# Writing out the first rounds and the last rounds of a software pipeline: gated attention and a GAT layer over 64 graphs

## The chip, the cores and the metric

The kernel runs on one core of a Trainium2 chip. The metric is the device time of one execution in microseconds, the median of several runs. Engines are named as in the profile: PE (TensorE, matrix products), DVE (VectorE), ACT (ScalarE), POOL (GpSimd) and SP (SyncE, which here issues the DMA transfers). Each engine works through its own queue in order.

## What is computed

There are 64 graphs of 256 nodes with 512 features (`x`: 64 x 256 x 512) and an adjacency matrix each (`adj`: 64 x 256 x 256). Two layers, each with a residual:

```python
# layer 0: gated multi-head attention, 8 heads of 64
h = maximum(layernorm(x), 0)
q, k, v = h @ Wq.T, h @ Wk.T, h @ Wv.T
attn = softmax(where(adj != 0, q @ k.T / 8, -inf))
c = attn @ v
gate = sigmoid(concat([c, h]) @ Wg.T + bg)
x = x + gate * h + (1 - gate) * c
# layer 1: GAT
h = maximum(layernorm(x), 0)
Wh = h @ W
e = leaky_relu((Wh @ a1)[:, :, None] + (Wh @ a2)[:, None, :], 0.2)
attention = softmax(where(adj == 0, -1e9, e))
x = x + elu(attention @ Wh)
```

## The kernel before

All is in float32. A graph passes through the pipeline in four groups of steps, named by their first letter and by the round in which they run. In round `i` the kernel does the preparation of graph `p = i + 1` (`p_`), the attention of graph `i` (`a_`), gate and first half of the GAT layer of graph `q = i - 1` (`g_`), the GAT product and softmax of graph `r = i - 2` and the last elementwise steps and the store of graph `o = i - 3`. `emit_round` (L650) writes the order of these steps by hand; that order is the order of every engine's queue, because the kernel is built under a manual schedule (L814): nothing reorders it. `do(fn, g, ...)` leaves a step out when graph `g` doesn't exist, and so the rounds at both ends (-1, 0, 1, ... and 63 to 66) are the same list with holes in it.

The five large products of a graph (q/k together, v, gate, wh; L158 `strassen`) are done with seven block products instead of eight. A product is a list of steps: "1" to "7" are block products on PE into three PSUM banks (`ma`, `mb`, `mc`, one buffer each), "u1", "u2", "u3" are partial sums and "c00" to "c11" the results, on DVE or ACT (L185, L187). Bank a holds steps 1 and 2, bank b 6, 7 and 4, bank c 5 and 3; a step that adds to a bank whose partial sum is still to be read waits for that read. `run(fn, g, "1 u1 6 ...")` in `emit_round` spreads these steps over the round and remembers which of them are done. The operands' token sums (L146, four additions on POOL) come before a product, weight sums (L104, four on DVE a weight) once, at the start, some of them as "chores" spread over the first rounds.

The steps that matter here:

- `load_graph` (L89): x and adj of a graph, on SP. `load_weight` (L99): two DMAs of 512 KB a weight; at the start wq and wv go on SP, wk on ACT's queue.
- `p_stats`, `p_root`, `p_bias`, `p_norm` (L224 to L233): layernorm and relu; statistics on DVE, the root on POOL, the norm on ACT.
- `p_turn`, `p_send`, `p_fetch` (L257 to L269): transposes h to hT. For graphs 0 and 1 on PE with an identity matrix (`transpose_pe`, L275), then copies to SBUF on DVE and ACT. From graph 2 on: 32 x 32 blocks on DVE, then a DMA to DRAM and back, both issued on SP.
- `p_qk` (L303), `p_v` (L321), `a_scores` (L328): q/k and v products, and the 8 heads' scores, partly into banks b and c.
- `a_max` (L349, DVE), `a_exp` (L358, ACT), `a_scale` (L367, POOL for three quarters, ACT for one), `a_turn` (L379, DVE), `a_send` and `a_fetch` (SP, L399 and L404): softmax and transpose of the weights; `eT` is what is fetched. `a_weigh` (L410): attention times v, on PE; `a_evac` (ACT).
- `g_gate` (L442), `g_diff` (POOL), `g_tanh` (ACT), `g_mix` (DVE): the gate. `g_turn`, `g_residual`: back to rows and added to x. For graphs from `LAST` = 62 on, PE does the transposes.
- `g_stats` to `g_norm`, `g_turn_h`, `g_sums_h`, `g_wh` (L546): layer 1's norm and product. `g_edges` (L552, PE), `g_logits`, `g_leaky` (DVE), `g_exp` (ACT), `g_turn_e` (L587, from graph 61 on by PE): its softmax. `g_out` (L611, PE): attention times Wh.
- `g_neg` (DVE), `g_pos` (ACT, two activations), `g_elu` (DVE), `g_add` (L635, POOL), `g_store` (L639, SP): elu, residual, store.

Before the rounds, L814 to L822 load graph 0 and wq, wk, wv, and normalise and transpose graph 0. The kernel's rounds -1 to 66 follow.

Of the kernel before, what the change touches and what calls it, by code (L numbers as in the profile page):

```python
# [8 lines left out]
F32 = mybir.dt.float32  # L9
# [3 lines left out]
ALU = mybir.AluOpType  # L13
# [9 lines left out]
def kernel(  # L23
# [32 lines left out]
    nc = tc.nc  # L56
    B, N, H = x.shape
# [4 lines left out]
    NT = N // P  # L62
    HH = H // 2
    SCALE = 1.0 / DK ** 0.5
    LAST = B - 2
    assert N == 256 and H == 512 and SCALE == 0.125

    def pool(name, bufs, **kw):
# [20 lines left out]
    def load_graph(g):  # L89
        xt = sb["x"].tile([P, NT, H], F32, tag="t", name=f"x_{g}")  # L90
        at = sb["adj"].tile([P, NT, N], I32, tag="t", name=f"adj_{g}")
        nc.sync.dma_start(xt, x[g].rearrange("(t p) h -> p t h", p=P))
        nc.sync.dma_start(at, adj[g].rearrange("(t p) n -> p t n", p=P))
        graphs[g] = {"x": xt, "adj": at}

    weight = {}
    sources = {"q": wqT, "k": wkT, "v": wvT, "gc": wgT[:H], "gh": wgT[H:], "1": w1}

    def load_weight(key, eng):  # L99
        w = weight[key] = const.tile([P, HC, 2, HH + (key == "1")], F32, name=f"w{key}_sb")  # L100
        for n in range(2):
            eng.dma_start(w[:, :, n, :HH], sources[key][:, n * HH:(n + 1) * HH].rearrange("(c p) f -> p c f", p=P))

    def weight_sums(key):  # L104

        w = weight[key]
        t = const.tile([P, 3, 2, w.shape[3]], F32, name=f"w{key}_t")
        b11, b12, b21, b22 = (w[:, r:r + 2, n, :] for r in (0, 2) for n in range(2))
        weight[key] = {1: b11, 2: b21, 3: b22, 4: t[:, 2], 5: b12, 6: t[:, 0], 7: t[:, 1]}
        return [lambda args=args: nc.vector.tensor_tensor(*args) for args in (  # L110
            (t[:, 1], b22, b12, ALU.subtract),
            (t[:, 0], t[:, 1], b11, ALU.add),
            (b12, b12, b11, ALU.subtract),
            (t[:, 2], b21, t[:, 0], ALU.subtract),
        )]
# [140 lines left out]

    def p_turn(g):  # L257

        if g == 1:
            p_transpose_pe(g)  # L260
        elif g > 1:
            turn(graphs[g]["h"])

    def p_send(g):
        s = graphs[g]
        if g > 1:
            s["there"] = send_blocks(s.pop("h").rearrange("p t h -> p (t h)"), f"h_{g}")

    def p_fetch(g):  # L269
        s = graphs[g]  # L270
        if g > 1:
            s["hT"] = sb["hT"].tile([P, NT, HC, P], F32, tag="t", name=f"hT_l0_{g}")
            fetch_blocks(s["hT"], s.pop("there"))

# [129 lines left out]
    def a_fetch(g, half, jj):  # L404
        s = graphs[g]
        eT = sb["e"].tile([P, 4, 4 * NT, 32], F32, tag="t", name=f"eT_{g}_{half}_{jj}")
        fetch(eT.rearrange("p a n c -> p a (n c)"), s.pop(("there", half, jj)))
        s["eT", half, jj] = eT.rearrange("p a (i t k) c -> p i k t a c", i=2, t=NT)
# [15 lines left out]
    def a_evac(g, half):  # L424
        s = graphs[g]
        if half == 0:
            s["cT"] = sb["cT"].tile([P, NT, HC, P], F32, tag="t", name=f"cT_{g}")
        nc.scalar.copy(  # L428
            s["cT"][:, :, 2 * half:2 * half + 2, :].rearrange("p t j q -> p j t q"),
            s["pc"].rearrange("p j (t q) -> p j t q", q=P),  # L430
        )

    def a_sums(g):
        s = graphs[g]
        s["cS"] = token_sums(s["cT"], f"c_{g}")


    def g_sums(g):
        s = graphs[g]
        s["hS"] = token_sums(s["hT"], f"g_{g}")  # L440
# [61 lines left out]
    def g_residual(g, t):  # L502
        s = graphs[g]
        x = s["x"][:, t, :]
        if g >= LAST:
            nc.vector.tensor_tensor(x, x, s["py"][t], ALU.add)
        else:
            x = x.rearrange("p (j i c) -> p j i c", i=4, c=32)
            nc.vector.tensor_tensor(x, x, s["yT"][:, :, t].rearrange("p i j c -> p j i c"), ALU.add)

    def g_stats(g, t):
        norm_stats(graphs[g], t, f"l1_{g}")

    def g_root(g):
        norm_root(graphs[g], f"l1_{g}")

    def g_bias(g):
        norm_bias(graphs[g], f"l1_{g}")

    def g_norm(g):  # L520
        graphs[g]["h1"] = norm_relu(graphs[g], f"l1_{g}")
# [23 lines left out]

    def g_wh(g):  # L546
        s = graphs[g]
        s["wh"] = sb["wh"].tile([P, NT, 2, HH + 1], F32, tag="t", name=f"wh_{g}")
        dst = [[s["wh"][:, t, n, :] for n in range(2)] for t in range(2)]
        return strassen(f"wh_{g}", [P, HH + 1], on_tokens(weight["1"], s["h1S"]), dst)  # L550

    def g_edges(g):  # L552
        s = graphs[g]
        pe = s["pe"] = ps["w"].tile([P, N], F32, tag="t", name=f"pe_{g}")
        for t in range(NT):
            nc.tensor.transpose(pe[:, t * P:(t + 1) * P], s["wh"][:, t, 1, HH:].to_broadcast([P, P]), ident)

    def g_logits(g):
        s = graphs[g]
        e = s["eg"] = sb["tmp"].tile([P, NT, N], F32, tag="t", name=f"eg_{g}")  # L560
        for t in range(NT):
            nc.vector.scalar_tensor_tensor(
                e[:, t, :], s["pe"], s["wh"][:, t, 0, HH:], s["mask"][:, t, :], ALU.add, ALU.add
            )

    def g_leaky(g):
# [44 lines left out]
    def g_out(g, t):  # L611
        s = graphs[g]
        pm = s["po", t] = ps["w"].tile([P, H], F32, tag="t", name=f"po_{g}_{t}")
        for kc in range(NT):
            nc.tensor.matmul(  # L615
                pm, s["egT"][:, t, kc, :], s["wh"][:, kc, :, :HH], start=(kc == 0), stop=(kc == NT - 1)
            )

    def g_neg(g, t):
# [14 lines left out]

    def g_add(g, t):  # L635
        s = graphs[g]
        nc.gpsimd.tensor_tensor(s["x"][:, t, :], s["x"][:, t, :], s.pop(("pos", t)), ALU.add)  # L637

    def g_store(g):  # L639
        nc.sync.dma_start(out[g].rearrange("(t p) h -> p t h", p=P), graphs[g]["x"])  # L640


    products = {}
# [2 lines left out]
    def chore(steps, n):  # L646
        for _ in range(min(n, len(steps))):
            steps.pop(0)()

    def emit_round(i):  # L650
# [4 lines left out]
        def do(fn, g, *args):  # L655
            if 0 <= g < B:
                fn(g, *args)

        def run(fn, g, steps):
            if 0 <= g < B:  # L660
                if (fn, g) not in products:
                    products[fn, g] = fn(g), set()
                product, done = products[fn, g]
                for step in steps.split():
                    if step not in done:
                        product(step)
                        done.add(step)

        tail = i >= B - 1

        run(g_gate, q, "1")
        do(g_neg, o, 1)
        do(p_send, p)
# [9 lines left out]
        run(g_gate, q, "6 u2")  # L683
        do(a_turn, i, 0, 1, 1)
        do(a_send, i, 0, 1)
        do(g_sums_h, r)
        do(g_elu, o, 0)
        run(g_gate, q, "5")
        do(a_scale, i, 1, 0)
# [27 lines left out]
        do(g_mix, q, 1, False)  # L717
        chore(chores, 2)
        run(g_wh, r, "2 c00 4")
        do(p_sums, p)  # L720
        do(g_turn, q)
        do(g_send, q)
        do(a_fetch, i, 0, 1)
        run(g_wh, r, "c10 3 c01")
        do(g_fetch, q)
        do(a_fetch, i, 1, 0)

# [33 lines left out]
        chore(chores, 1)  # L761
        do(g_stats, q, 0)
        if i == -1:
            chore(weight_sums("v"), 4)
        run(p_v, p, "1 u1 6 u2")
        do(g_stats, q, 1)
        do(g_root, q)
# [2 lines left out]
        do(g_norm, q)  # L770
        run(p_v, p, "2 c00")
        chore(chores, 1)
        if not tail:
            do(g_turn_h, q)
            do(g_send_h, q)
        run(p_v, p, "4 c10")
        chore(chores, 1)
        run(p_v, p, "3 c01")
        chore(chores, 1)
        do(p_stats, p + 1, 0)  # L780
        do(p_stats, p + 1, 1)
        do(p_root, p + 1)
        do(g_sums, i)
        if tail:
            do(g_out, r, 0)
            do(g_out, r, 1)
            do(g_turn_h, q)

        do(a_weigh, i, 0)
        do(a_evac, i, 0)  # L790
        do(a_weigh, i, 1)
        do(a_evac, i, 1)
        do(a_sums, i)
        do(a_scores, p, 0)
        do(a_scores, p, 1)
        if not tail:
            do(g_out, r, 0)
            do(g_out, r, 1)
        do(a_max, p, 0, 0)
        do(p_bias, p + 1)  # L800
        do(a_exp, p, 0, 0, 0)
        do(a_max, p, 0, 1)
        do(a_exp, p, 0, 0, 1)
        do(p_norm, p + 1)
        do(a_max, p, 1, 0)
        do(a_max, p, 1, 1)
        do(g_fetch_h, q)
        do(a_scale, p, 0, 0)
        do(a_exp, p, 0, 1, 0)
        do(a_exp, p, 0, 1, 1)  # L810
        do(g_neg, r, 0)
        do(p_turn, p + 1)

    with tc.manual_schedule(engines={getattr(mybir.EngineType, e) for e in ("PE", "SP", "Pool", "DVE", "Activation")}):  # L814
        load_graph(0)
        load_weight("q", nc.sync)
        load_weight("k", nc.scalar)
        load_weight("v", nc.sync)
        p_stats(0, 0)
        p_stats(0, 1)  # L820
        for fn in (p_root, p_bias, p_norm, p_transpose_pe):
            fn(0)  # L822
        for i in range(-1, B + 3):
            emit_round(i)
            graphs.pop(i - 3, None)


# [30 lines left out]
```

## Time and profile before

| what | value |
|---|---|
| median of 3 runs | 3191.97 us (3191.17 to 3193.47) |
| the profiled execution's own time | 3185.72 us |
| its span on the core | 3183.9 us |
| PE busy | 3125.0 us (98% of the span) |
| PE weight loads busy | 2723.9 us (86%) |
| DVE, ACT, POOL busy | 2467.8, 1413.6, 1506.3 us (78%, 44%, 47%) |
| first matrix instruction on PE | 9.24 us |
| end of the last POOL addition, issue of the last store | 3180.06, 3180.08 us |

A row of the timeline reads: start in us, duration in us, engine, source line, operation, what it writes <- what it reads, shape, count; in brackets how long the engine had been idle and what released it. A row of waits reads: who waited, for whom, us in total, how many times, the longest. In a row of stages the busy time of each engine is followed by its number of instructions; the last three numbers are the clock granted to PE (1.00 is full), the share of the DMA engines and GB/s. Because PE is busy nearly throughout, what other engines do matters where PE waits for it.

### The profile page before, as it was taken

To read this page: it belongs to the slowest core of one execution; us is meant where nothing else is said; L and a number is where in the kernel's file an instruction comes from. 1 tells how busy PE (TensorE), PEld (TensorE's weight loads), DVE (VectorE), ACT (ScalarE), POOL (GpSimd) and SP (SyncE) were. 2 spreads that over 40 slices of the span, in tenths; PEclk is the share of its full clock that TensorE was granted. 3 is DMA by queue.
4 is the path that set the end of the run, shared out by engine and by line. 5 is a ranking of instruction groups with operands and counts; after the bars stand their busy time and mean duration, and the time that the engine had idled before them with its cause. 6 is when DMAs were issued, how large, how long until landed. Compare 5 with 4: busy or idle time off the path is not lost.

```text
span 3183.9 us, 66670 instructions
## 1 busy us (share of the span) xinstructions
PE 3125.0 (98%) x22716; PEld 2723.9 (86%) x22716; DVE 2467.8 (78%) x6366; ACT 1413.6 (44%) x3976; POOL 1506.3 (47%) x2183
## 2 busy tenths in 40 slices
PE   7899999999999999999999999999999999999997
PEld 6888888888889888888888898888888888888984
DVE  6777877877877878778778778778787787787774
ACT  2343543543544534435435445445344344454442
POOL 2454544544544545535445445445454454454453
PEclk9999999999999999999999999999999999999998
DMA  5678778777777777787787777777877877877761
GB/s 169 176 173 204 189 180 206 185 180 206 182 190 199 184 191 195 180 203 187 178 211 184 181 207 182 190 197 177 200 189 182 205 186 179 211 183 183 204 170 44
DMA packets 1103394, 590.63 MB, mean 186 GB/s; under 512 B 685776, under 2 KB 1029328, under 8 KB 1103056
## 3 DMA queue, kind: packets, MB, share of 16 engines
q1 hardware_dynamic: 1102000, 585.32, 73.9%
q8 instruction: 182, 2.98, 0.4%
q14 instruction: 156, 1.28, 0.1%
q10 hardware_dynamic: 1056, 1.05, 0.1%
HBM read 304.88 MB, written 281.28 MB: 184 GB/s over the span
## 4 chain that ended last, share of the span: by engine, by line
PE 90%; DVE 4%; POOL 2%; DMA 2%; issue 1%; SPq 1%; ACT 0%; DVEq 0%; POOLq 0%; ACTq 0%
PE pmb_qk L174 11%; PE pmb_z L174 9%; PE pc L418 7%; PE pma_qk L174 7%; PE pmc_qk L174 7%; PE ps L338 6%; PE po L615 6%; PE pma_z L174 6%; PE pmc_z L174 6%; PE pmb_v L174 5%; PE pmb_wh L174 5%; PE pma_v L174 3%; PE pmc_v L174 3%; PE pmc_wh L174 3%; PE pma_wh L174 3%; DVE e L353 1%
## 5 line engine op out<-in xcount | busy, mean ns | idle before, releaser
L362 ACT ACTIVATE e<-e,low 128x256 f32<-128x256 f32 x1024 | 506.5, 499 | 63.3 <-DVE low L353 63.3
L204 POOL TENSOR_TENSOR rs_l<-ve_l,mhalf 128x2 f32<-128x2 f32 x128 | 89.0, 695 | 869.7 <-DVE ve_l L200 869.7
L353 DVE CUSTOM_DVE_ANT_0 e<-ps,mask 128x256 f32<-128x256 f32 x1024 | 362.1, 415 | 100.1 <-PE ps L338 100.1
L377 POOL TENSOR_SCALAR e<-e,rec 128x256 f32<-128x256 f32 x768 | 352.7, 477 | 148.8 <-DVE rec L370 100.4
L386 DVE STREAM_TRANSPOSE eb<-e 128x512 f32<-128x512 f32 x512 | 351.8, 696 | 76.7 <-POOL e L377 63.4
L213 ACT ACTIVATE h_l<-x,nb_l,rs_l 128x512 f32<-128x512 f32 x256 | 194.1, 805 | 212.4 <-DVE nb_l L208 123.5
L152 POOL TENSOR_TENSOR S_l<-hT_l 128x256 f32<-128x256 f32 x128 | 93.4, 730 | 395.9 <-DMA hT_l<-there_h 361.9
L637 POOL TENSOR_TENSOR x<-x,pos 128x512 f32<-128x512 f32 x128 | 160.1, 1272 | 229.3 <-DVE pos L633 229.3
L615 PE MATMUL po<-wh,egT 128*128 128x512 f32 x512 | 242.5, 617 | 2.1 <-ACT egT L598 2.1
L338 PE MATMUL ps<-qk 64*128 64x256 f32 x2048 | 238.9, 383 | 0.6 <-DVE v L185 0.6
L418 PE MATMUL pc<-eT,v 128*64 128x256 f32 x2048 | 235.9, 382 | 0.1
L338 PEld LDWEIGHTS ps<-qk 64*128 64x128 f32 x2048 | 193.1, 187 | 45.3 <-DVE ve_l L200 21.9
L418 PEld LDWEIGHTS pc<-eT,v 128*64 128x64 f32 x2048 | 141.3, 137 | 86.7 <-DMA eT<-there_e 16.3
L239 DVE STREAM_TRANSPOSE h_l<-h_l 128x512 f32<-128x512 f32 x248 | 167.8, 695 | 54.7 <-ACT h_l L213 54.7
L615 PEld LDWEIGHTS po<-wh,egT 128*128 128x128 f32 x512 | 94.3, 194 | 118.5 <-issue 95.1
L362 ACT ACTIVATION_READ_ACCUMULATOR e<-e,low 128x1 f32 x1024 | 194.8, 190 | 0.0
L196 DVE BATCH_NORM_STATS2 bs_l<-x 128x6 f32<-128x512 f32 x256 | 172.9, 675 | 5.4 <-DMA x<-in_x_dram 5.4
L461 ACT ACTIVATE z<-z,hbg 128x256 f32<-128x256 f32 x256 | 116.1, 502 | 105.9 <-DVE z L185 105.9
L456 POOL TENSOR_TENSOR d<-hT_l,cT 128x512 f32<-128x512 f32 x128 | 160.5, 1274 | 0.0
L428 ACT COPY cT<-pc 128x512 f32<-128x512 f32 x128 | 74.9, 585 | 184.5 <-PE pc L418 184.5
L174 PEld LDWEIGHTS pma_z<-hT_l,wgh_sb 128*128 128x128 f32 x1024 | 129.2, 192 | 30.4 <-issue 30.4
L174 PE MATMUL pma_qk<-hT_l,wq_sb 128*128 128x128 f32 x1024 | 139.6, 280 | 11.9 <-DMA hT_l<-there_h 10.1
(146 smaller groups left out, 7964.8 us busy)
## 6 DMA issues: line engine op xcount, KB each, us to landing
there_e<-eb SPq DMA_DIRECT2D x256, 512.0 KB, 3.4
eT<-there_e SPq DMA_DIRECT2D x1024, 128.0 KB, 3.9
there_h<-h_l SPq DMA_DIRECT2D x496, 128.0 KB, 3.3
hT_l<-there_h SPq DMA_DIRECT2D x496, 128.0 KB, 3.3
x<-in_x_dram SPq DMA_DIRECT2D x64, 512.0 KB, 4.0
out_dram<-x SPq DMA_DIRECT2D x64, 512.0 KB, 4.2
there_y<-y SPq DMA_DIRECT2D x62, 512.0 KB, 3.3
yT<-there_y SPq DMA_DIRECT2D x248, 128.0 KB, 3.4
```

Source lines behind the costliest of these rows:

```text
L174: nc.tensor.matmul(bank[key][(slice(None), *cols)], lhsT, rhs, start=first and i == 0, stop=last and i == len(todo) - 1, skip_group_check= ...
L196: nc.vector.bn_stats(bs, s["x"][:, t, :])
L213: nc.scalar.activation(h[:, t, :], s["x"][:, t, :], AF.Relu, bias=s["nb"][:, t:t + 1], scale=s["rs"][:, t:t + 1])
L239: nc.vector.transpose(h[:, t, :], h[:, t, :])
L338: nc.tensor.matmul(psc[jj, i][:, t, :], qk[r:r + DK, 0, jj, t * P:(t + 1) * P], qk[r:r + DK, 1, jj, :], start=True, stop=True,)
L353: nc.vector.tensor_tensor_reduce(s["e", half, jj][:, i, t, :], s["ps", half][jj, i][:, t, :], s["mask"][:, t, :], -SCALE, HUGE, ALU.add, A ...
L362: nc.scalar.activation(e, e, AF.Exp, bias=s["low", half][:, jj, i, t:t + 1], scale=-1.0, accum_out=s["sums", half][:, jj, i, t:t + 1],)
L377: nc.gpsimd.tensor_scalar(e, e, rec[:, i, t:t + 1], 1.0, ALU.mult, ALU.mult)
L386: nc.vector.transpose(s["eb", half, jj][:, :, 4 * i:4 * i + 4, :].rearrange("p b n c -> p n b c"), e)
L418: nc.tensor.matmul(pc[i * DK:(i + 1) * DK, jj, :].rearrange("p (t a c) -> p t a c", t=NT, c=32), s["v"][:, kc, hd * DK:(hd + 1) * DK], eT[ ...
L456: nc.gpsimd.tensor_tensor(d, s["hT"][:, :, js, :], s["cT"][:, :, js, :], ALU.subtract)
L615: nc.tensor.matmul(pm, s["egT"][:, t, kc, :], s["wh"][:, kc, :, :HH], start=(kc == 0), stop=(kc == NT - 1))
```

## The change

In the front:

- SP loads x of graph 0, wq, wk, then adj of graph 0, then wv; ACT's queue issues no load. While x loads, PE transposes the identity matrix 44 times into a PSUM tile that nobody reads (`wake_up`).
- The sums of wv are done on POOL.
- In round -1, statistics of graph 1 and the scores and softmax of graph 0 are put ahead of the product v of graph 0.
- In round 0, the token sums of graph 1 come first, and its products q/k and v stand in the places of gate and wh, which that round doesn't have.
- Graph 2 is transposed on PE too (`FIRST` = 3).

At the end, round 63 stops after the product wh of graph 61, and `emit_end` writes out all that is left, for graphs 60 to 63. The additions of graphs 60 to 63 go to DVE. In graph 63 the additions are two (x + pos, then + (neg - 1)), and each half is stored on its own. Its wh has two tiles of its own, in buffers that held q and k. Rounds 1 to 62 keep their order.

```diff
+        if g > 0:
+            load_edges(g)
+
+    def load_edges(g):
+        nc.sync.dma_start(graphs[g]["adj"], adj[g].rearrange("(t p) n -> p t n", p=P))
...
     def p_turn(g):
-        if g == 1:
+        if g < FIRST:
             p_transpose_pe(g)
...
     def g_add(g, t):
         s = graphs[g]
-        nc.gpsimd.tensor_tensor(s["x"][:, t, :], s["x"][:, t, :], s.pop(("pos", t)), ALU.add)
+        eng = nc.vector if g >= B - 4 else nc.gpsimd
+        eng.tensor_tensor(s["x"][:, t, :], s["x"][:, t, :], s.pop(("pos", t)), ALU.add)
+    def g_add_first(g, t):
+        s = graphs[g]
+        nc.vector.tensor_tensor(s["x"][:, t, :], s["x"][:, t, :], s["pos", t], ALU.add)
+    def g_add_last(g, t):
+        x = graphs[g]["x"][:, t, :]
+        nc.vector.scalar_tensor_tensor(x, graphs[g].pop(("neg", t)), -1.0, x, ALU.add, ALU.add)
...
         def run(fn, g, steps):
+            if fn is g_gate and i == 0:
+                fn, g = p_qk, p
+            elif fn is g_wh and i == 0:
+                fn, g = p_v, p
...
+        if i == 0:
+            do(p_sums, p)
         run(g_gate, q, "1")
...
-        do(p_sums, p)
+        if i != 0:
+            do(p_sums, p)
         do(g_turn, q)
         do(g_send, q)
         do(a_fetch, i, 0, 1)
         run(g_wh, r, "c10 3 c01")
+        if i == B - 1:
+            return
...
         if i == -1:
-            chore(weight_sums("v"), 4)
+            chore(weight_sums("v", nc.gpsimd), 4)
+            stats()
+            scores()
         run(p_v, p, "1 u1 6 u2")
...
+    def wake_up():
+        pt = ps["w"].tile([P, 4, P], F32, tag="t", name="awake")
+        for k in range(44):
+            nc.tensor.transpose(pt[:, k % 4, :], ident, ident)
+
+    def emit_end():
+        a, b, c, o = B - 1, B - 2, B - 3, B - 4
+        a_fetch(a, 1, 0)
+        a_fetch(a, 1, 1)
+        g_edges(c)
+        for t in range(NT):
+            g_residual(b, t)
+            g_stats(b, t)
+        g_root(b)
+        g_bias(b)
+        g_sums(a)
+        g_norm(b)
+        for half in range(2):
+            a_weigh(a, half)
+            a_evac(a, half)
+        g_turn_h(b)
+        a_sums(a)
+        g_logits(c)
+        g_leaky(c)
+        gate = g_gate(a)
+        for step in "1 u1 6 u2 5".split():
+            gate(step)
+        g_exp(c)
+        g_sums_h(b)
+        g_elu(o, 1)
+        g_add(o, 1)
+        g_add(o, 0)
+        g_store(o)
+        g_rec(c)
...
+        g_out(c, 0)
+        g_out(c, 1)
+        g_turn(a)
+        wh = g_wh(b)
...
+        for t in range(NT):
+            g_residual(a, t)
+            g_stats(a, t)
+        g_root(a)
+        for step in "6 u2 5".split():
+            wh(step)
+        g_bias(a)
+        g_norm(a)
+        for step in "7 u3 c11 2 c00 4 c10 3 c01".split():
+            wh(step)
+        g_edges(b)
+        g_turn_h(a)
+        g_sums_h(a)
+        g_logits(b)
+        g_leaky(b)
+        last = g_wh(a)
...
+        for t in range(NT):
+            g_elu(c, t)
+            g_add(c, t)
+        g_store(c)
+        for step in "7 u3 c11 2 c00".split():
+            last(step)
...
+        for t in range(NT):
+            g_elu(b, t)
+            g_add(b, t)
+        g_store(b)
+        for t in range(NT):
+            g_neg(a, t)
+            g_pos(a, t)
+            g_add_first(a, t)
+        for t in range(NT):
+            g_add_last(a, t)
+            g_store(a, t)
...
         load_graph(0)
         load_weight("q", nc.sync)
-        load_weight("k", nc.scalar)
+        load_weight("k", nc.sync)
+        load_edges(0)
+        wake_up()
         load_weight("v", nc.sync)
...
-        for i in range(-1, B + 3):
+        for i in range(-1, B):
             emit_round(i)
-            graphs.pop(i - 3, None)
+            graphs.pop(i - 4, None)
+        emit_end()
```

## The prediction

> **What bounds the kernel now.** I first cut the span into three stages at the score products of round 2 and of round 62, with the busy time of each engine and the granted clock (the last three columns are clock, DMA share and GB/s):
>
> ```profile
> span 3183.9 us, 66670 instructions
> ...
> core 0: us, PE busy (x) PEld busy (x) DVE busy (x) ACT busy (x) POOL busy (x), PEclk, DMA share, GB/s
> 0.00:171.80 171.80, 141.06 (x1024) 126.33 (x1024) 117.94 (x305) 56.83 (x162) 53.27 (x90) 0.96 0.63 172
> 171.80:3079.90 2908.10, 2903.75 (x21244) 2538.07 (x21242) 2297.17 (x5935) 1319.91 (x3720) 1413.12 (x2044) 1.00 0.77 190
> 3079.90:3183.90 104.00, 80.21 (x456) 59.46 (x454) 52.73 (x126) 36.84 (x94) 39.88 (x50) 0.90 0.24 70
> ```
>
> TensorE is full between the ends, at full clock, and only its waits count. One graph costs it, by the chain of work: q/k and gate 7 x 1.79 = 12.5 us each, v and wh 6.07 each, scores 3.65, weighing 3.60, edges 0.45, output product 3.64: 48.5; two weighings in the middle start 48.29 apart. Up to 171.8 it has done 4 q/k, 4 v, 3 scores, 3 weighings, 2 gates, one wh, one edges and 16 transposes (1.8): 129.4 us, so the front loses 42.4. After 3079.9, 71.3 us of such work remain (two gates 25.0, three wh 18.2, three edges 1.3, four output products 14.6, scores and weighing 7.2, 44 transposes 5.0): the end loses 32.7. The middle loses 2908.1 - 60 x 48.29 = 10.7. The change can only reach for 75 us.
>
> Then who TensorE waited for, in the front and in the end (us, times, longest):
>
> ```profile
> PE pt_l L281 <- ACT h_l L213: 11.2, 4, 9.2
> PE pma_qk L174 <- DMA hT_l<-there_h: 6.3, 2, 6.0
> PE pmb_qk L174 <- POOL S_l L153: 4.0, 1, 4.0
> ```
> ```profile
> PE ptr L596 <- ACT eg L578: 9.6, 4, 3.2
> PE po L615 <- ACT egT L598: 2.1, 3, 0.7
> ```
>
> The front waits for its first input, for hT of graph 2 by DMA, for token sums of graph 1 behind two head scalings on POOL. The end waits three times for a GAT softmax. The clock by stretches shows what waits cost further:
>
> ```profile
> 39.03:42.44 3.41, 2.07 (x15) 1.00 0.01 2
> 42.44:45.85 3.41, 1.63 (x12) 1.00 0.00 0
> 45.85:49.26 3.41, 2.98 (x15) 0.50 0.28 114
> 3107.57:3110.98 3.41, 0.32 (x2) 1.00 0.25 49
> 3110.98:3114.40 3.42, 2.68 (x6) 0.50 0.00 0
> 3114.40:3117.80 3.40, 3.40 (x5) 0.50 0.95 286
> ```
>
> The clock changes on a 3.41 us grid: a stretch with 1.6 us of work or less is followed by half clock (about 1.7 us lost each, where TensorE is the limit), one with 2.07 was not; 2.68 us did not end a half-clock stretch, 2.98 did.
>
> **First loads and the 44 transposes.** x shares the DMA engines with adj, wq, wk and wv and is used at 5.37. Alone in front it gains between 0 and 1.4 us (its usual landing is 4.0 after issue at 0.72); I take 0.8. The transposes start when ident is written (1.3 us). At half clock one costs about 0.21 us (8 matmuls in 1.67 to 1.87), at full clock 0.11. The Trainium skill speaks against them ("TensorE: Matmul & The Clock Gate", section "Part 4: PE-mode transpose"): transposes don't count as busy for the clock gate in the way that products do. Then they run 44 x 0.21 = 9.4 us until 10.7, keep the array from h (ready 8.5) and put hT about 1 us later than before. If they count, the clock rises after one or two stretches, they end near 8.6, the eight real transposes cost 0.9 instead of 2.2, and hT comes about 1.3 earlier. No stretch above decides it (the one at 42.44 held transposes mostly, but too little work of either kind). Eight transposes take 1.03 us at full clock and eight matmuls 1.06: by that nearest row I let them count, -1.3, with +1.0 as the other end. hT only frees VectorE's weight sums: TensorE waits for the second wk sum (17.86). wk moves from ACT's queue to SP's behind wq, adj behind both, wv last: 2.75 MB by about 10 us at the 348 GB/s of those first microseconds, in time. wv's four sums move to POOL (4 x 1.27 = 5.1 from about 16), while VectorE's wk sums run; beside POOL such a sum took 1.13 to 1.22 instead of 0.69: +0.5. q/k of graph 0 ends at 27.2 instead of 27.95.
>
> **Scores before v.** Scores(0) start after q/k (36.8 becomes 28.0); statistics of graph 1 (1.75 us) go first on VectorE, sixteen maxima of 0.345 end at 36. v(0) then shares a PSUM bank with the last scores: its step 6 waits until 35.3 (2.4 us of TensorE), its u1 for eight exponentials and a norm on ACT; it ends at 40.8, where it ended at 36.2. hT(1) is there at 42.8 instead of 45.4.
>
> **Round 0.** POOL now does the token sums of graph 1 first; scaling (0, jj 1) waits behind them for hT(1), 42.8 + 2.9 = 45.8 to 47.6 (before: 48.5). q/k(1) and v(1) run while heads are scaled, turned and sent, which removes the 4.0 us wait and two half-clock stretches, but u2, u3, c11 of q/k now stand between VectorE's turns: the last of four sends goes at about 55.7, where it went at 53. SP then issues 16 fetches and graph 2's loads (10 us): the last weights land at 69.1. TensorE, done with v(1) at 62, waits for them, in two pieces of about 2 and 3.5 us, and is likely to fall to half clock once (1.5). Scores(1) start at 70.9 instead of 74.9. A new wait has replaced the old ones: gain 4.0.
>
> **Graph 2 transposed on TensorE.** Eight transposes, 0.9 us, behind its norm on ACT (4 exponentials, 1.5 us): TensorE reaches them at 76.1 with the half clock and leaves at 77.0. Meanwhile the bank that gate step 6 waited for (1.0 us) is free. So the gate runs 77.0 to 90.9 (before 78.6 to 93.5). Then nothing waits for hT(2): the 6.0 us and the 2.25 of half clock behind it (q/k start 3.75 + 2.08 instead of 3.58) are gone. Late next: VectorE's mixes, chores and turns last 6.5 us beyond the gate, u2 of q/k(2) stands behind them, and step 7 waits 1.8. Weighing(1) comes at 90.9 + 18.6 + 1.8 = 111.3 instead of 120.4; its fetches are there, 19.9 after the gate. Front: -9 us; between -3 (transposes don't count, two more half-clock stretches) and -15 (no cold stretch, u2 in time).
>
> **Rounds 3 to 62.** Their code, queue order and tiles are the same: 0.
>
> **The end.** The walk starts at 3107.0, after wh(61). Before, SP issued the last eT fetch at 3114, behind the store of graph 60 and POOL's adds; now at 3106, landing at 3111.4. VectorE does residual and statistics of graph 62 first (3.1 us), so norm(62) ends at 3113.1 (before 3117.7) and logits(61) slip from 3108 to 3114.6, which nobody needs yet. Weighing(63) ends at 3113.3, transposes 3114.2, gate(63) 3127.1 with the 0.5 of exp(61)'s transposes inside (before 3136.3). Output(61) to 3130.8, py 3131.7; step 7 of wh(62) waits 1.3 for u2 behind residual and statistics of 63. wh(62) ends 3139.0, edges and transposes 3141.0. wh(63) waits 1.0 for POOL's token sum and about 1.0 for u3, which stands behind four VectorE adds and elus of graph 61 (2.6): ends 3150.1 (before 3163.0). Output(62) 3151.2 to 3154.9 hides the softmax of 63, output(63) runs 3156.2 to 3159.8 at full clock (3.6 instead of 5.3). VectorE then owes elu and add of 62 (2.6) before it may start on 63: its last add ends at 3165.5, then 3.8 us for the store, as here:
>
> ```profile
> 3177.58 2.48 POOL L637 TENSOR_TENSOR x<-x,pos 128x512 f32<-128x512 f32 x2 [8.01 <-DVE pos L633]
> 3180.08 0.37 SPq L640 DMA_DIRECT2D out_dram<-x  x1
> ```
>
> End 3169.4: -14.5; between -9 (three in-order waits of 2 us that I miss) and -18 (no wait).
>
> **The sum.** The profiled execution took 3185.72, its span and 1.8; the median is 6.3 above it. The saving, 9 + 14.5 = 23.5, is taken off the median: 3191.97 - 23.5 = 3168.5, I say 3168.
>
> **The rivals.** (1) Both ends as walked: 3168, own range 3163 to 3174. Chance 0.57. (2) Round 0 gives the front back: weights wait longer, TensorE falls cold twice more (front -2): 3191.97 - 16.5 = 3175.5. For it: sends leave later than before. Against: 12 us of waits are removed by name. 0.19. (3) The waits I put in vanish, front -15 and end -17: 3160. 0.13. (4) The end's VectorE order blocks TensorE, end -5: 3178. 0.06. (5) Slower: the middle. Only 7 of 60 rounds wait for hT there, 3.8 us in all, longest 1.0. If the new front left each round's fetch late against TensorE, the price is up to 1.0 x 60 - 23.5 = +36.5 (3228); it decides from 0.4 us a round. Against it: SP's order in a round is unchanged, and TensorE's own pace sets the next round. 0.03. (6) The gains cancel, within 0.2% (6.4 us, about what a measurement of this kernel can tell from no change): 0.02. So faster 0.95, same 0.02, slower 0.03. The range takes in (2), (3) and (4): 3159 to 3181.
>
> **What would show it.** Right: q/k(2) follows the gate of graph 0 without a wait for hT; a TensorE wait for eT near 62 to 69; weighing starts 48.3 apart as before; no 3 us waits for exp in the end; full clock in the last output product. Wrong: 0.21 us transposes to the end of the 44; half clock beyond 10 us in the front; middle rounds above 48.5; a VectorE-held TensorE wait over 2 us in the end.

## The result, and the profile after

The changed kernel takes 3178.36 us (median of 6 runs, 3171.57 to 3179.17), the kernel before 3191.57 on the same chip (6 runs, 3190.14 to 3193.47): ratio 0.9955, 95% interval 0.9942 to 0.9967. That is 13 to 14 us where 23.5 were forecast. The profiled execution took 3178.26 us, its span is 3176.5.

The three stages of the changed kernel, cut at the same products as before (scores of round 2, scores of round 62):

```profile
span 3176.5 us, 66771 instructions
...
core 0: us, PE busy (x) PEld busy (x) DVE busy (x) ACT busy (x) POOL busy (x), PEclk, DMA share, GB/s
0.00:174.10 174.10, 147.66 (x1075) 131.11 (x1075) 117.68 (x300) 57.31 (x163) 59.74 (x94) 0.95 0.59 164
174.10:3087.50 2913.40, 2904.87 (x21242) 2537.34 (x21240) 2296.91 (x5935) 1321.12 (x3720) 1416.02 (x2044) 1.00 0.77 190
3087.50:3176.40 88.90, 73.04 (x456) 56.64 (x454) 58.81 (x134) 36.71 (x94) 31.26 (x42) 0.97 0.28 82
```

The end is 15 us shorter (104.0 before, 89.0 to the end of the span), as forecast. The front isn't shorter at all: its mark moved from 171.8 to 174.1, where about 163 was forecast. The middle reads 5.3 us longer in this profile; over the profiles of the table below it lies anywhere from 2908 to 2919, and at 2909.1 when the changed kernel is profiled again (a1). The medians say the same: take the two ends and the 1.8 us outside the span off them, and 2914.0 is left for the middle before and 2913.5 after. So those 5.3 are no effect.

Whom TensorE waited for in the front of the changed kernel (us, times, longest):

```profile
PE pc L423 <- DMA eT<-there_e: 5.4, 3, 3.1
PE pmb_qk L179 <- DVE wk_t L115: 4.9, 1, 4.9
PE pmb_qk L179 <- DVE u_qk L190: 2.8, 1, 2.8
PE pmb_v L179 <- DVE qk L190: 2.3, 1, 2.3
PE pmb_v L179 <- DVE low L358: 2.1, 1, 2.1
```

and in its end:

```profile
PE pmb_wh L179 <- DVE u_wh L190: 1.8, 2, 1.3
PE pe L569 <- DVE wh L190: 1.6, 3, 0.5
PE pc L423 <- DMA eT<-there_e: 1.3, 2, 0.7
PE pmb_wh L179 <- POOL S_l L158: 1.1, 1, 1.1
PE po L628 <- ACT egT L611: 0.7, 1, 0.7
```

The old waits for hT of graph 2, for token sums of graph 1 and for the exps of the end are gone. The wait for the input is only filled: the first transpose of h starts at 9.20 us (9.24 before), behind 44 transposes that nobody reads. In the end nothing longer than 1.3 us has come in their place; in the front a new list has, 17.5 us in these five rows. The clock joins in: I added up the time at half clock from stretches of 1 us over the front (twice what the granted clock lacks to 1.00). Every sum is close to a multiple of 3.41, the grid that the prediction had read. It counts only what the clock column shows: the first products of a kernel run slowly too (eight in 2.08 us in g3), in rows that still read 1.00.

| kernel | scores(0) | scores(1) | scores of round 2 | at half clock in the front | end | time, ratio to before [95%] |
|---|---|---|---|---|---|---|
| before | 36.8 | 74.9 | 171.8 | 13.7 | 104.0 | 3191.57 |
| changed | 34.8 | 78.9 | 174.1 | 17.1 | 89.0 | 3178.36, 0.9955 [0.9942, 0.9967] |
| a1 (changed, again) | 33.3 | 79.4 | 174.1 | 17.1 | 89.0 | 3178.35, 0.9959 [0.9945, 0.9972] |
| e1 | 30.0 | 78.5 | 173.1 | 20.5 | 89.3 | 3176.01, 0.9944 [0.9933, 0.9956] |
| e2 | 31.4 | 78.0 | 174.0 | 23.9 | 89.4 | 3176.82, 0.9946 [0.9934, 0.9958] |
| e3 (end alone) | 37.1 | 75.6 | 172.5 | 20.5 | 89.5 | 3177.52, 0.9947 [0.9935, 0.9959] |
| e5 | 37.6 | 76.6 | 173.1 | 20.5 | 105.5 | 3193.22, 0.9997 [0.9989, 1.0005] |
| g2 | 33.5 | 79.4 | 173.5 | 20.5 | 89.4 | 3179.92, one run |
| g3 | 33.0 | 79.4 | 174.3 | 13.7 | 89.0 | 3176.10, one run |
| g4 | 33.7 | 79.9 | 176.9 | 23.9 | 89.0 | 3183.04, one run |
| h1 | 31.5 | 73.2 | 168.9 | 13.7 | 89.0 | 3171.59, one run |
| g1 | 31.3 | 72.1 | 165.5 | 13.6 | 89.0 | 3170.85, 0.9932 [0.9919, 0.9946] |
| h2 | 29.2 | 69.1 | 163.0 | 6.8 | 88.9 | 3167.76, 0.9926 [0.9913, 0.9938] |
| h3 | 33.3 | 79.5 | 173.4 | 17.1 | 88.2 | 3177.41, one run |

The times scatter by several us from run to run, and the profile of before was 6 us below its own median. The marks are the sharper tool: in the two profiles of the changed kernel the end agrees within 0.1 us. In the front they scatter more. The changed kernel, a1 and h3 have the same front, and its last mark comes at 174.1, 174.1 and 173.4; scores(0) come at 34.8 in one and at 33.3 in the other two. So under 1 us at the last mark is no difference.

### The profile page after: what moved, and what is told of

Its sections match the earlier page's. It is cut to its first block, busy times and chain, and to the rows that moved or that the text cites. A ratio compares the mean times of both kernels' runs of the same rounds, so it can differ in the third digit from the quotient of the medians.

```text
span 3176.5 us, 66771 instructions
## 1 busy us (share of the span) xinstructions
PE 3125.6 (98%) x22768; PEld 2725.1 (86%) x22768; DVE 2473.4 (78%) x6369; ACT 1415.1 (45%) x3977; POOL 1507.0 (47%) x2179
## 4 chain that ended last, share of the span: by engine, by line
PE 88%; DVE 5%; DMA 3%; POOL 2%; SPq 1%; issue 1%; ACT 1%; DVEq 0%; ACTq 0%; POOLq 0%
PE pmb_qk L179 10%; PE pmb_z L179 9%; PE pma_qk L179 7%; PE pmc_qk L179 7%; PE pc L423 7%; PE ps L343 6%; PE pma_z L179 6%; PE pmc_z L179 6%; PE po L628 6%; PE pmb_v L179 5%; PE pmb_wh L179 5%; PE pmc_v L179 3%; PE pma_v L179 3%; PE pmc_wh L179 3%; PE pma_wh L179 3%; DVE e L358 1%
## 5 line engine op out<-in xcount | busy, mean ns | idle before, releaser
L651 POOL TENSOR_TENSOR x<-x,pos 128x512 f32<-128x512 f32 x120 | 150.2, 1273 | 184.2 <-DVE pos L646 184.2
L433 ACT COPY cT<-pc 128x512 f32<-128x512 f32 x128 | 74.9, 586 | 189.8 <-PE pc L423 189.8
```

## The experiments

**First question: does the collision of DVE and POOL cost the front its gain?** In the changed kernel the sums of wv on POOL run at the same time as the sums of wk on DVE, and both are slower. DVE, then POOL (start, duration, line, what):

```profile
17.59 1.74 DVE L115 TENSOR_TENSOR wk_t<-wk_sb 128x512 f32<-128x512 f32 x1
19.36 1.64 DVE L115 TENSOR_TENSOR wk_t<-wk_t,wk_sb 128x512 f32<-128x512 f32 x1
20.92 1.76 DVE L115 TENSOR_TENSOR wk_sb<-wk_sb 128x512 f32<-128x512 f32 x1
```
```profile
17.20 1.59 POOL L115 TENSOR_TENSOR wv_t<-wv_t,wv_sb 128x512 f32<-128x512 f32 x1
```

The theory (A) was that this wait of 4.9 us, and the half clock behind it, ate the front's gain. The rival (B): scores(1) are set by round 0's late sends and fetches, and an earlier start is lost there.

e1, in the changed kernel:

```diff
-            chore(weight_sums("v", nc.gpsimd), 4)
+            chore(weight_sums("v"), 4)
```

> The changed kernel with one part undone: the four weight sums of v go back from POOL to DVE, at the same place. Marks: start of graph 0's scores (before 36.8 us, changed 34.8) and start of the scores of round 2 (before 171.8, changed 174.1). Theory A (the front's gain is lost because POOL's sums of v slow DVE's sums of wk from 0.69 to 1.7 us each, so that TensorE waits 4.9 us and falls to half clock): that wait shrinks to about 1 us, scores(0) start near 28.5 and, with 2.8 us more on DVE before the maxima, the scores of round 2 start at 166 to 170; time 4 to 8 us below the changed kernel. Rival B (the order of round 0 itself loses it: TensorE waits for fetched weights however early the scores are): scores(0) come earlier but the scores of round 2 start at 172 or later; time within 2 us of the changed kernel.

e2, the sums stay on POOL, behind the statistics:

```diff
-            chore(weight_sums("v", nc.gpsimd), 4)
             stats()
+            chore(weight_sums("v", nc.gpsimd), 4)
             scores()
```

> The changed kernel with the four weight sums of v still on POOL, but put behind the statistics of graph 1 (POOL's root of graph 1 waits for DVE, so the sums begin near 29 us, after DVE's sums of wk). Theory A (contention between POOL's and DVE's sums, not POOL's slower sum, is the loss): wk's sums take 0.7 to 1.2 us again, the wait for wk falls from 4.9 to about 1 us, scores(0) start near 28.5, v's step 6 (waiting for a PSUM bank until 35 anyway) hardly waits for the sums (end near 35), and the scores of round 2 start at 164 to 168; time 6 to 10 us below the changed kernel. Rival B (round 0's order): 172 or later, time within 2 us. Rival C (POOL is too slow for these sums anywhere): v of graph 0 waits for them more than 3 us and the scores of round 2 start later than in the kernel with the sums on DVE.

In e2 the same instructions take their usual time:

```profile
16.37 0.68 DVE L115 TENSOR_TENSOR wk_t<-wk_sb 128x512 f32<-128x512 f32 x1
17.08 0.69 DVE L115 TENSOR_TENSOR wk_t<-wk_t,wk_sb 128x512 f32<-128x512 f32 x1
```
```profile
34.40 1.27 POOL L115 TENSOR_TENSOR wv_t<-wv_sb 128x512 f32<-128x512 f32 x1
```

The wait for wk falls from 4.9 to 1.3 (e1) and 1.8 us (e2). Scores(0) start 4.8 and 3.4 us earlier than in the first profile of the changed kernel, 3.3 and 1.9 us earlier than in its second (a1). Yet scores of round 2 come at 173.1 and 174.0, hardly outside the 173.4 to 174.1 of this front. The collision is real, and it is not what the front lacks: A fell.

Where did e2's 1.9 us against a1 go? TensorE waits 2.7 us for the maxima of the scores instead of 2.1, and does v(0) from step 6 on in 6.9 us, as in a1 (half clock in both). The rest is still there at scores(1) and at the end of the gate of graph 0 (1.4 us at both), so round 0 passes the gain on. It goes behind the gate. There VectorE waits for the transposed output of the gate, `yT`, before it can do the residual of graph 0. In e2 that residual starts only 0.3 us earlier than in a1 (115.86), since the fetches of `yT` took 5.7 us to land instead of 4.3 (medians):

```profile
115.55 0.69 DVE L514 TENSOR_TENSOR x<-x,yT 128x512 f32<-128x512 f32 x1 [3.88 <-DMA yT<-there_y]
```
```profile
122.88 3.67 PE L423 MATMUL pc<-eT,v 128*64 128x256 f32 x32
```

The second row is weighing(1). It follows this residual by 7.33 or 7.34 us in nine profiles: changed, a1, e1, e2, g1, g2, g3, h1 and h3. Whether TensorE came to v(2) through a wait (a1) or through two half-clock stretches in q/k(2) (e2) makes no difference. So B, as it was put, fell here too: this start was lost behind round 0, at a transfer that neither theory named.

e5 makes this one part alone in the kernel before (`weight_sums("v", nc.gpsimd)` at the old place).

> The kernel before with one part of the change alone: the four weight sums of v on POOL. Theory A: POOL starts them right behind graph 0's token sums, they run beside DVE's sums of wk and stretch these to about 1.7 us each; TensorE's wait for wk grows from 1.6 to about 5 us and half clock follows; the wait for v's sums (1.9) goes. Scores(0) start 2 to 4 us later than before (36.8), time 2 to 5 us above before. Rival B (that part costs nothing, the loss is round 0's order): scores(0) start up to 2 us earlier and the time is 0 to 2 us below before.

The wait for wk grew from 1.6 to 3.3 us, the wait for v's sums (1.9) vanished, scores(0) came at 37.6 instead of 36.8. Ratio 0.9997 [0.9989, 1.0005]: no change that can be measured.

**Second: is the end worth its 15 us alone?** e3 is the kernel before with the changed end only: `emit_end`, the additions on DVE, two wh tiles for graph 63; the front, its loads and its queue order as before.

> One half alone: the end as changed (emit_end, adds on DVE, two tiles for the last wh), the front as before (loads, rounds -1 to 2, graph 2 by DMA, sums of v on DVE). If front and end are independent, the scores of round 2 start at 171.8 as before, the stretch from the scores of round 62 to the end of the span is 89 us as in the changed kernel (before 104.0), and the time is 15 us below before. Theory A and B both expect it to be about as fast as the changed kernel or up to 3 us faster. A rival, that the end's gain depends on the new front: the stretch would be above 95.

The end takes 89.5 us, the time ratio is 0.9947 [0.9935, 0.9959]. All of the change's gain is here; that the rest of the change saves time can't be seen (0.9955 and 0.9959 with it).

**Third: what does round 0 cost?** SP's queue in the changed kernel (start, duration of the whole group, line, what):

```profile
50.52 11.49 SPq L397 DMA_DIRECT2D there_e<-eb  x4
62.19 5.90 SPq L402 DMA_DIRECT2D eT<-there_e  x12
68.32 0.40 SPq L92 DMA_DIRECT2D x<-in_x_dram  x1
68.98 0.40 SPq L98 DMA_DIRECT2D adj<-in_adj_dram  x1
69.52 2.11 SPq L402 DMA_DIRECT2D eT<-there_e  x4
```

Four sends take 11.5 us (6.1 before), and nothing is fetched until the last has left, though the first two quarters could be. Then 16 fetches and graph 2's loads go out in 9.4 us. From 70 to 75 us the DMA engines are full while TensorE is busy for 2.17 us of 5, and 75 to 80 it is at half clock (last three columns: clock, DMA share, GB/s):

```profile
65.00:70.00 5.00, 4.42 (x24) 3.14 (x22) 3.50 (x10) 0.37 (x1) 0.00 (x0) 1.00 1.03 227
70.00:75.00 5.00, 2.17 (x16) 1.14 (x16) 3.73 (x13) 0.59 (x1) 0.00 (x0) 0.96 1.09 271
75.00:80.00 5.00, 3.02 (x14) 1.72 (x16) 0.61 (x3) 0.59 (x1) 3.82 (x6) 0.50 0.18 36
```

TensorE's rows show the price: the last quarter of the weighing waits 3.05 us and runs at half clock (eight products in 1.98 us; in g1 in 1.08), and so do most of the scores behind it (4.97 us; 3.7 in g1):

```profile
76.98 1.98 PE L423 MATMUL pc<-eT,v 128*64 128x256 f32 x8 [3.05 <-DMA eT<-there_e]
78.88 4.97 PE L343 MATMUL ps<-qk 64*128 64x256 f32 x32
```

g1 is e2 with each quarter fetched behind the send that follows its own in round 0 (the last two behind the last send), and x of graph 2 loaded a round earlier (its adj stays in place):

```diff
         do(a_send, i, 0, 1)
+        if i == 0:
+            do(a_fetch, i, 0, 0)
...
         do(a_send, i, 1, 0)
+        if i == 0:
+            do(a_fetch, i, 0, 1)
...
         do(a_send, i, 1, 1)
+        if i == 0:
+            do(a_fetch, i, 1, 0)
+            do(a_fetch, i, 1, 1)
...
             load_small()
+            load_graph(2)
```

> The changed kernel with the sums of v behind the statistics of graph 1 (as in e2) and another order of the SP queue in round 0: each quarter of graph 0's weights is fetched right behind the send after it instead of all sixteen fetches behind the last send, and graph 2's x is loaded in round -1, where SP is idle from 21 to 50 us. No other engine's order changes. Theory B1 (what eats the front is the tail of DMA work behind the last send: 2 MB of fetches and 0.75 MB of loads from 62 to 77 us, with the DMA engines full from 65 to 75): the last quarter lands at 66 to 69 us instead of 77, weighing(0) waits under 1 us, no half clock there, scores(1) start at 70 to 73 (changed 78.9), scores of round 2 at 165 to 169 (changed 174.1); time 5 to 9 us below the changed kernel. Rival B2 (the sends themselves are late, because the turns stand between the evacuations of q/k, and nothing behind them matters): scores(1) at 76 or later, time within 2 us.

SP's queue in g1, and the one wait for weights that is left:

```profile
49.37 4.95 SPq L397 DMA_DIRECT2D there_e<-eb  x2
54.41 2.22 SPq L402 DMA_DIRECT2D eT<-there_e  x4
58.34 0.34 SPq L397 DMA_DIRECT2D there_e<-eb  x1
58.79 2.79 SPq L402 DMA_DIRECT2D eT<-there_e  x4
61.68 0.38 SPq L397 DMA_DIRECT2D there_e<-eb  x1
62.91 4.60 SPq L402 DMA_DIRECT2D eT<-there_e  x8
```
```profile
PE pc L423 <- DMA eT<-there_e: 1.0, 1, 1.0
```

The last send leaves about as late as in the changed kernel (61.7), but eight of the sixteen fetches are out by then. The wait falls from e2's 5.6 to 1.0 us, three of seven half-clock stretches are gone, and scores of round 2 come at 165.5: 8.5 us better than e2 (6.0 of them at scores(1), the rest behind it). In this B holds: the order of fetches and loads around round 0 is worth more than any other edit to the front that was tried. h1 splits it: g1 without the early x.

> The kernel with early fetches in round 0, but graph 2's x loaded in its old place again. The changed kernel with late sums of v (e2) reaches the scores of round 1 at 78.0 and of round 2 at 174.0, with both edits at 72.1 and 165.5. Theory B1 says that the tail behind the last send is DMA work of any kind (2 MB of fetches, 0.75 MB of loads): the fetches alone give two thirds to three quarters, scores of round 2 at 167 to 169. Rival: x alone is what matters (its late landing holds the statistics, and these the norm and transposes of graph 2): 171 or later.

Scores of round 2 at 168.9: the fetches are worth 5.0 us, x another 3.5.

g2 restores the old order of round 0 in the changed kernel (q/k, v and the token sums of graph 1 go back behind the scaling of heads).

> The changed kernel with one part undone: in round 0 q/k and v of graph 1 stand in their old places again and the token sums of graph 1 in theirs; all else as changed (loads, 44 transposes, scores before v, graph 2 on TensorE, end). Theory B (this part only moves TensorE's work ahead of the wait for graph 0's weights, and its evacuations delay the sends): the four sends go out within 6 us instead of 11.5, the last near 56 instead of 62, scores(1) start between 75 and 79 as in both kernels, scores of round 2 within 2 us of the changed kernel's 174.1. If the part is worth what was claimed, scores(1) start at 82 or later.

The sends take 5.8 us again, and the wait for token sums comes back as 4.2 us (`POOL S_l`). Scores of round 2: 173.5 against 174.1. That part of the change trades a 4.2 us wait for a 5.4 us wait; by this one profile it is worth nothing as it stands.

**Fourth: what are the other parts of the front worth?** g3 leaves out `wake_up()`.

> The changed kernel without the 44 transposes. If they only raise the clock for the eight transposes of graph 0 and the first q/k steps: these are slow again (0.21 instead of 0.11 us each), q/k of graph 0 starts 0.4 to 0.7 us later than at 11.2, and nothing behind DVE's weight sums moves: scores(0) start at 34.5 to 35.5 (changed 34.8), the scores of round 2 within 1 us of 174.1. Rival (the early warm clock carries on): scores(0) 2 us later or more.

Scores of round 2 come at 174.3 (174.1 with it): nothing. g4 sets `FIRST = 2`, so graph 2 goes by DMA again.

> The changed kernel with graph 2 transposed by DVE and DMA again, as before. By the prediction's step (6.0 us of waiting and 2.25 of half clock saved) the scores of round 2 start 7 to 9 us later than 174.1. Rival: DVE holds q/k(2) up anyway (u2 stands behind the mixes and turns of graph 0, v's step 6 behind a residual that waits for yT), so that most of the wait for hT(2) is hidden there: 1 to 4 us later.

The wait for hT(2) is back (5.3 us), and yet scores of round 2 come only 2.8 us later, at 176.9. Without it TensorE waits 2.8 us for u2 of q/k(2) and 2.3 us in v(2); with it, neither is among its waits. The second largest wait of the front before was worth half of its length, because VectorE's results for the same products came hardly earlier.

**Last: the best of these, and the additions at the end.** h2 is g1 without `wake_up`, and with w1's weight sums of round 1 moved behind u2 of q/k(2) (the first line stands in two places, both are changed):

```diff
-        chore(chores, 2)
+        chore(chores, 2 if i != 1 else 0)
...
-        wake_up()
```

> The kernel with early fetches and early x, without the 44 transposes, and with the four weight sums that stand on DVE in round 1 ahead of u2 of q/k(2) moved behind it. If u2 waits for DVE's backlog, the 2.9 us wait of step 7 falls below 1 us and the scores of round 2 start at 161 to 164 (165.5 before these two edits); the missing transposes cost nothing (within 0.5 us). If the backlog is the mixes and turns alone, 165 to 166. Time 20 to 27 us below before and 8 to 13 us below the changed kernel.

It takes 3167.76 us, ratio 0.9926 [0.9913, 0.9938]; the changed kernel, on the same chip, 0.9959 [0.9945, 0.9972]. The intervals don't overlap: h2 is about 10.6 us faster than the change and 23 faster than before. Its front ends at 163.0, where the prediction had put it, but with edits that the prediction did not have. What the two extra edits did apart was not tried. The trace of h2 hints at it: at scores(0) it is 2.1 us ahead of g1, since it stayed at full clock in q/k(0) (g1, with the transposes, fell), but at the end of the gate of graph 0 only 0.6 us. Behind the gate, with the sums out of VectorE's way, the residual starts 13.3 us after the gate instead of 16.2. The wait for u2 vanished, and waits of 1.2, 0.7 and 0.6 us in v(2) took back part; at the last mark 2.5 us are left.

h3 leaves the additions of graphs 60 to 62 on POOL (`eng = nc.gpsimd`); graph 63 keeps its two on VectorE.

> The changed kernel with one part of its end undone: the residual additions of graphs 60 to 62 on POOL again (graph 63 keeps its two additions on DVE). The prediction's walk has four DVE operations of graph 61 (2.6 us) hold u3 of the last wh by about 1 us, and elu and add of graph 62 hold graph 63's last steps. If so, the stretch from the scores of round 62 to the end is 1 to 2.5 us shorter than 89.0. Rival (POOL's 1.27 us an addition and its hand-over cost more than DVE's backlog): 1 us longer or more.

The end takes 88.2 us: 0.8 less, since VectorE no longer has two additions ahead of u3 of wh(63). The 0.55 us wait there is gone. Right in direction, smaller than the 1 to 2.5 expected. a1 is the changed kernel again, to go with h1 to h3.

> The changed kernel once more, beside the others on one chip. Scores of round 2 within 1 us of 174.1, stretch from the scores of round 62 to the end within 1 us of 89.0, and the stretch between the two, 2913.4 in its first profile against 2908.1 in that of before, between 2908 and 2918: if it scatters so, the 5.3 us between the first two profiles are no effect of the change.

## Why the prediction was right in direction and wrong in size

**The end (-14.5; measured -15.0): right, step by step.** Counted from scores of round 62, output(63) was walked to start at 76.3 and started at 76.6; the last addition was walked to end at 85.6 and ended at 85.9. The wait for u2 behind residual and statistics of 63: 1.3 forecast, 1.26 measured; POOL's token sum 1.0 and 1.12; u3 behind the additions 1.0 and 0.55. The last output product ran at full clock:

```profile
3164.11 3.70 PE L628 MATMUL po<-wh,egT 128*128 128x512 f32 x8 [0.73 <-ACT egT L611]
...
3172.08 1.29 DVE L660 SCALAR_TENSOR_TENSOR x<-neg,x 128x512 f32<-128x512 f32 x2
...
3172.79 0.95 SPq L665 DMA_DIRECT2D out_dram<-x  x2
```

**The middle (0):** right. e3, with the old front, has the same middle within the scatter, so rival (5) has nothing to show.

**The front (-9; measured +2.3 by the profiles, about 0 by the times of e3 and the changed kernel): wrong.** Two steps failed: hT(1) came 6.4 us too late, and from scores(1) to weighing(1) the kernel took 3.9 us more than forecast. The case that came is nearest to rival (2), "round 0 gives the front back", and worse than it was priced (-2). That the time is rival (4)'s (3178) is chance: its mechanism, a blocked end, didn't come. By steps:

- *Transposes of the identity (-1.3).* Here they do count for the clock. TensorE in two stretches of the changed kernel, in which only they run (busy, count, clock, DMA share, GB/s):

```profile
0.00:6.30 6.30, 4.95 (x23) 1.00 0.73 205
6.40:8.70 2.30, 2.30 (x22) 1.00 1.09 355
```

  From 1.35 to 6.3 one takes 0.215 us, from 6.4 on 0.105: full clock after transposes alone. The Trainium skill says that full clock does not engage for transpose mode ("TensorE: Matmul & The Clock Gate", "Part 4: PE-mode transpose"); the profile lists these instructions as MATMUL and does not show a mode, so whether they are what the page means stays open. The clock column reads 1.00 in both rows: before its first recorded change it says nothing, the durations do. But the gain is not used: behind the transposes TensorE waits for VectorE's sums, and loses the clock again. g3 shows nothing gained by them.
- *x alone in front (-0.8):* statistics start at 5.32 instead of 5.37. Nothing.
- *v's sums on POOL (+0.5):* DVE's sums took 1.64 to 1.76 us, not the 1.13 to 1.22 I had from a row beside smaller POOL operations, and POOL's own 1.59 to 1.72, not 1.27. The wait became 4.9 us, and three half-clock stretches cover it and the products behind it. q/k(0) ended at 33.9 instead of 27.2. (In a1 it ended at 32.4, with half clock in v(0) instead; hT(1) came no earlier.) The wait is the largest miss where it stands, and worth at most 1 us at the end of the front (e1, e2): without it hT(1) is still 5.3 us behind the forecast in e2, 3.4 of it by scores(0), with two half-clock stretches in q/k(0), and 1.9 in v(0), with one.
- *Scores before v, and round 0 (-4 at scores(1); measured +4).* Walked from its own start, this step was nearly right: v(0) waited 2.1 us (2.4 forecast); last send 12.8 us after hT(1) (12.9 forecast); the last weights used 15.0 us after that (13.4 forecast); three waits of 5.4 us in all (5.5 forecast). So the step failed by its start (hT(1) at 49.2 instead of 42.8) and by 1.7 us behind the last send. That the weights would be late was on the list; that it was the dearest line of the front, and could be moved by the order of SP's queue alone (g1), was not.
- *"Likely to fall to half clock once (1.5)".* I had priced one half-clock stretch in the new front; there are five, 17.1 us in all (13.7 before), and six or seven in e1, e2, g2 and g4. By the products that ran in them they cost the changed kernel about 5 us: 2.8 in q/k(0), which I had put at nothing, and 2.1 in the last quarter of the weighing and scores(1). My own sign ("wrong: half clock beyond 10 us in the front") came true. In e1 and e2 a shorter wait for wk came with more half clock, in g1, h1 and h2 a later stage without waits came with less. But time at half clock is not time lost at the end of the front: e2's two stretches in q/k(2) stand where a1 waits for VectorE, and e3, with the front of the kernel before and two stretches more, has its last mark only 0.7 us later. The clock can't be set by an edit, so how much of g1's and h2's gain is clock and how much is wait stays open.
- *Graph 2 on TensorE (from scores(1) to weighing(1) 40.4; measured 44.3).* The wait for hT(2) vanished as forecast. Late next was u2, as forecast, but 2.8 us instead of 1.8. Not foreseen: v(2)'s step waits 2.3 us for a q/k result that stands on VectorE behind the residual of graph 0, which itself waits for its transposed output by DMA:

```profile
115.86 0.69 DVE L514 TENSOR_TENSOR x<-x,yT 128x512 f32<-128x512 f32 x1 [5.10 <-DMA yT<-there_y]
116.47 0.68 DVE L190 TENSOR_TENSOR qk<-pmb_qk,u_qk 128x512 f32<-128x512 f32 x1
```

  VectorE stood idle for 5.1 us, with the result that TensorE needed next in its queue behind the residual. This is the step that failed here: the prediction had no line for `yT`, and by the nine profiles above its landing sets weighing(1), 24.7 us after the end of the gate where 20.4 were forecast. Before, q/k(2) itself came so late that VectorE found `yT` there (no wait at 111.00), so the wait for hT(2) had hidden it; without that wait 2.8 us were won (g4) of the 8.25 that the prediction counted. The wait of step 6 in the gate of graph 0 (1.0 us) did vanish, as forecast. I had asked what is late next, and stopped at the first answer.

Of the 11.9 us by which weighing(1) was later than forecast (123.2 instead of 111.3), 6.4 were there at hT(1), 1.7 came between last send and scores(1), 3.9 behind scores(1). The sum of the terms measured, +2.3 - 15.0 = -12.7, is close to what the runs show (-13.2).

## What to carry to other kernels

In a start-up phase where every engine waits in turn, removing a wait is worth only the distance to the next one, and the idle time that the next one leaves may cost the clock as well; so follow each removed wait, on every engine whose results TensorE needs, until TensorE has run a whole stage unhindered. Reckon with half clock behind long waits: in the fronts of these kernels it followed every wait of 3.4 us or more, and of the shorter ones some and not others (the 2.1 us wait in v(0) had none behind it in the changed kernel's first profile and one in a1). Ask first what the in-order queue of transfers does: here two moves of DMA issues in round 0 (fetch each quarter behind the next one's send, load x a round earlier) gave 8.5 us, more than all the front's parts of the change together. An end with few free choices can be walked to half a microsecond, and it pays to test it alone.

## What the runs showed of the hardware that was not expected

- Two-input float32 sums of 128x512 on DVE and POOL at once slow each other: DVE 0.69 to 1.64–1.76 us, POOL 1.27 to 1.59–1.72. The four POOL sums and the four DVE sums beside them took 7.3 us from first to last (15.4 to 22.7); one after the other, by e2's rows, they would take 5.1 and 2.6. Running them at once gained next to nothing. The Trainium skill names a cause that fits ("GPSIMD Engine Reference", "1. Specifications": the SBUF interfaces are shared with VectorE, with contention where a DVE instruction has two SBUF inputs); the numbers are these rows'.
- float32 transposes against the identity, with nothing else on TensorE, went from 0.215 to 0.105 us each from 6.4 us on, and so to full clock.
- x of graph 0 landed no earlier when it was issued alone in front (first use 5.32 instead of 5.37 us).
